# A macaron of attention and mixture-of-experts layers: the first grouped FFN in parts of 12, 12 and 8 token tiles, moments of the second attention between its slot tiles, and the expert search's counts in BF16

## The chip, the core and the metric

The kernel runs on one core of a Trainium2 chip. The metric is the device time of one execution in microseconds (us); the median of several executions is compared. PE is the matrix engine, PEld its weight load, DVE the vector engine, ACT the scalar engine, POOL the general engine that here mostly issues indirect DMAs, SP the engine that issues the other DMAs. All data are FP32 unless said otherwise.

## What is computed

4096 tokens (8 sequences of 512) of 256 numbers pass through six residual layers, in this order:

```python
x = x + 0.5 * ffn0(layernorm(x))   # 8 experts choose 512 tokens each of every 2048
x = x + attn0(layernorm(x))        # rope, 16 heads of 16, causal
x = x + 0.5 * ffn0(layernorm(x))
x = x + 0.5 * ffn1(layernorm(x))   # each token chooses 4 of 16 experts, plus a shared FFN
x = x + attn1(layernorm(x))        # 16 heads of 64, with its own inner residual
x = x + 0.5 * ffn1(layernorm(x))
```

In `ffn0` each expert takes the tokens with its highest scores (`top_k` over the tokens, for each half of the batch), runs them through 256-1024-256 with a GELU and adds them back weighted. In `ffn1` each token takes 2 of 4 groups of experts and then the 4 best experts:

```python
scores = softmax(x @ gate_w.T)
group_scores = scores.reshape(T, 4, 4).max(-1)
_, gidx = top_k(group_scores, 2)            # the others are masked
_, indices = top_k(masked, 4)
a = silu(x @ w1[e]) * (x @ w3[e])           # 256 -> 128
y = sum over the 4 experts of c[t, e] * (a @ w2[e])
z = (silu(x @ ws1) * (x @ ws3)) @ ws2       # shared, 256 -> 256 -> 256
```

## The kernel before

The 4096 tokens are 32 token tiles of 128 rows. The residual `x` stays in SBUF for the whole kernel. Six stages follow one another: `ffn0` until 583 us, `attn0` until 1285, `ffn0` again until 1838, `ffn1_before` until 2300, `attn1` until 3550, `ffn1_after` to the end. Within a stage the order of each engine's instructions is written out by hand (`manual_schedule`): instructions stand on each engine in the order of the Python calls, and the engines are strict queues. So what a change moves in the program moves on every engine that it touches.

**The search in `ffn0`.** The 512 best scores of each expert are found by a search for the threshold, two bits of the score a round (`search`, 8 and then 7 rounds). The scores lie as 128 rows of 256, 16 rows for each expert. In a round DVE compares all scores with two of three thresholds `thr` (L362, the results `junk` are thrown away, the counts go to `r`), ACT does the third by a sign; a matmul with the 0/1 matrix `same` sums the counts over the rows of an expert (`total`, L350, output `cnt`); DVE prepares `here` (L377) and `base` (L379), then turns the counts into a digit (`hit`, L384), the new thresholds (`thr`, L389) and the value found so far (`at`, L391). After the last round, ties are settled by two scans along the rows (`inc`, L421 and L428), and a matmul with `before` adds up the rows ahead of each row (`off`). `ffn0` normalizes its token tiles in groups of four (L254); some of these rows are POOL's.

**Layer norm.** `ln_moments` (L168, L169) takes mean and variance of one tile on DVE; `ln_finish` (L176 and on) turns the variances of several tiles into `rstd`, with a square root on ACT in the middle. The rows are then normalized one tile at a time.

**The grouped FFN** (`Grouped`, used as #1 before and #2 after the second attention). Tokens are sent to slots in HBM that are sorted by expert, 144 tiles of 128 slots. The tokens are handled in parts; #1 has four of 8 token tiles, #2 has three of 12, 8 and 12.

- `prepare(h)` works on part h: moments, finish, rows (`rows`, L1406, output `wide`), then for each group of four tiles the transposes (`tp`, L1687), the logits, and the way back to rows (L1708, L1713).
- `route(h)` takes the scores, the groups, the four experts and each row's slot, in one chain of DVE operations over all tiles of the part, with a few small matmuls (L1480, L1488, L1568) and ACT operations (L1444 the exponential) between.
- `send` (L1416) then issues four indirect DMAs for each token tile from POOL, one for each chosen expert; each moves 128 rows (128 KB) to their slots. A send waits until the send before the previous one has landed, so two are under way.
- `shared(g)` is the shared FFN of a group of four tiles (L1763, L1774, L1785), its last operation adds to `x` (L1791). `Pump` holds its units and issues them one by one.
- `tile_steps` gives `step(i)`: one slot tile moves on through a pipeline of turn (`tpx`, L1831; `xT`, L1833), hide (`hs`, L1849; `sgs`, L1855; `as`, L1857), back (L1861) and give (`yps`, L1869; `ys`, L1877 on ACT or L1879 on DVE), and the result is stored to `ys_d`. `load` brings four slot tiles (`xs`) from HBM. A slot tile belongs to a part once no later part can put rows into it; `closed[h]` slot tiles are closed after part h, and a load of such tiles waits for all sends of parts up to h. The rest wait for the last part. `ready[h]` is the number of slot tiles after which all results of part h are stored.
- `collect` gives a list of steps; each one gathers the four results of a token tile (`yg`, L1600, indirect DMA on POOL, four under way) and adds, two tiles behind, what was gathered (L1619 on DVE).

In `ffn1_before` (#1) the parts 0 and 1 are prepared, routed and sent ahead of the slot tiles, with the shared groups 0 to 3 in between; then the closed slot tiles of parts 0 to 1, and then 2, run with the routing and sending of parts 2 and 3 and the shared groups 4 to 7 beside them. From the slot tile `ready[0] + 6` on, one element of `collect` goes with each slot tile, until the first two parts are added. What is left goes into `attn1`. The weights of `attn1` (four loads of 1 MB) are issued in the same loop, one every eighth slot tile.

`attn1` begins with `ln_range` over its first 12 token tiles, that is their moments and the finish, then rows (`xn`, L1072) and transposes (`tpn`, L1084).

In `ffn1_after` (#2) the last part is prepared and routed first, since the earlier parts were sent during `attn1`; the slot tiles follow, with gathers alternately one and two at a tile; at the end the shared groups that are left run with the rest of the gathers and the output's DMAs.

Of the kernel before, what the change touches and what calls it, by code (L numbers as in the profile page):

```python
# [61 lines left out]
class Kernel:  # L62
    def __init__(self, ctx, tc, w):
# [44 lines left out]
        self.same = const.tile([P, P], F32, name="same")  # L108
# [10 lines left out]
        self.before = const.tile([P, P], F32, name="before")  # L119
# [89 lines left out]
    def ffn0(self, n, beside, known=0):  # L209


        with ExitStack() as ctx:
            E = mybir.EngineType
            with self.tc.manual_schedule(engines={E.PE, E.DVE, E.Activation, E.Pool}):
                self._ffn0(ctx, n, beside, known)

    def _ffn0(self, ctx, n, beside, known):
# [30 lines left out]
        def rows(g):  # L248
            xn = xns[g] = work.tile([P, QT, D], F32, name="xn", bufs=3)
            for i in range(QT):  # L250
                t = g * QT + i

                engine = nc.gpsimd if i == 3 or i == 1 and not known else nc.vector
                engine.tensor_scalar(  # L254
                    xn[:, i, :], self.x[:, t, :], mv[:, t, 0:1], rstd[:, t : t + 1], ALU.subtract, ALU.mult
                )
# [95 lines left out]
        def search(vals, rounds, between):  # L352
# [3 lines left out]
            at = None  # L356
            for b in range(rounds - 1, -1, -1):
                v = work.tile([P, D], F32, name="v", bufs=4)
                nc.scalar.mul(v, vals, 0.25 ** (b + 1))
                r = work.tile([P, 3], F32, name="r", bufs=2)  # L360
# [4 lines left out]
                nc.scalar.activation(signs, v, AF.Sign, bias=thr[:, 2:3], accum_out=r[:, 2:3])  # L365
                cnt = psum.tile([P, 3], F32, name="cnt", tag="psI", bufs=1)
# [20 lines left out]
                if b > 0:  # L387
                    thr = work.tile([P, 3], F32, name="thr", bufs=2)
                    nc.vector.scalar_tensor_tensor(thr, self.signs, digit[:, 0:1], base, ALU.mult, ALU.add)  # L389
                at = work.tile([P, 1], F32, name="at", bufs=4)  # L390
                nc.vector.tensor_scalar(  # L391
                    at, here, digit[:, 0:1], 0.0 if b > 0 else 0.5, ALU.add, ALU.add
                )
            return at
# [15 lines left out]
        sums = pool.tile([P, 2], F32, name="sums")  # L410
# [15 lines left out]
        nc.vector.tensor_tensor(gt, gt, eq, ALU.add)  # L426
# [3 lines left out]
        total(off, self.before, inc[:, D - 1 : D])  # L430
# [190 lines left out]
    def _attn0(self, ctx, weights):  # L621
# [353 lines left out]
        with tc.manual_schedule(engines={E.PE, E.DVE, E.Activation}):  # L975
# [22 lines left out]
            for g in range(G):  # L998
# [12 lines left out]
                if half == 1 and b > 0 and g % 6 < QT:  # L1011

                    self.ln_moments(pool, self.stats, (b - 1) * QT + g % 6, 1)
# [9 lines left out]
                finish(1)  # L1023
                do(mid)
# [25 lines left out]
    def _attn1(self, ctx, weights, beside, after):  # L1050
# [9 lines left out]
        stats = self.ln_tiles(pool)  # L1060
# [194 lines left out]

        E = mybir.EngineType
        with tc.manual_schedule(engines={E.PE, E.DVE, E.Activation, E.Pool}):
            self.ln_range(pool, stats, 0, 3 * QT)
# [92 lines left out]
class Grouped:  # L1351
# [58 lines left out]
    def send(self, h, t, row, behind=None):  # L1410
# [4 lines left out]
        for r in range(TOPK):  # L1415
# [5 lines left out]
            before = self.sent[-2:-1]  # L1421
            for other in before:
                tc.add_manual_dep(inst, other.name, SYNC, reason="two transfers at a time")
# [214 lines left out]


# [75 lines left out]
    def prepare(self, h):  # L1715
# [3 lines left out]
        for t in range(a, b, 2):  # L1719
            k.ln_moments(self.rpool, self.stats, t, 2)  # L1720
            yield
        k.ln_finish(self.rpool, self.stats, a, b - a)
        yield
        for t in range(a, b, 2):
            for i in range(t, t + 2):
                self.rows(k.nc.vector, self.xn[:, i, :], i)
            yield
# [12 lines left out]
    def send_next(self):  # L1740

        if self.waiting:
            h, t = self.waiting.pop(0)
            self.send(h, t, self.xn[:, self.base[h] + t, :], self.latest)
# [185 lines left out]
def ffn1_before(k, f):  # L1930
# [4 lines left out]
    with ExitStack() as ctx, k.tc.manual_schedule(engines={E.PE, E.DVE, E.Activation, E.Pool, E.SP}):  # L1935
# [6 lines left out]
        groups = [f.shared(g) for g in range(TT // QT)]  # L1942
        load, step, total = f.tile_steps()
        at = 0

# [3 lines left out]
        for h in range(2):  # L1949

            pair = groups[2 * h : 2 * h + 2]
            pump.feed(pair[0][0] + pair[1][0] + pair[0][1] + pair[1][1])
            routing, preparing, more = f.route(h), f.prepare(h + 1), True
            while more:
# [6 lines left out]
                more = f.send_next() or more  # L1961
        pump.flush()
        load(0)
        for h in (2, 3):
            one, two = groups[2 * h], groups[2 * h + 1]
            pump.feed(one[0] + two[0] + one[1] + two[1])
            routing, preparing, more = f.route(h), f.prepare(3) if h == 2 else iter(()), True
            while at < f.closed[h - 1] or more:
                if at < f.closed[h - 1]:
                    step(at)  # L1970
                    at += 1
                if at % 4 == 0 or at == f.closed[h - 1]:
                    pump.run(1)
                more = advance(routing, 2)
                more = advance(preparing, 1) or more
                pump.flush()
                more = f.send_next() or more
        while pump.units or pump.pending:
            pump.run(1)
        while at < f.closed[3]:  # L1980
            step(at)
            at += 1

        coming = f.collect()
        begin, weights = f.ready[0] + 6, None
        for i in range(at, total):
            step(i)
            if i >= begin and i % 8 == 0 and (weights is None or len(weights) < 4):
                weights = k.attn1_weights(weights)

            if i >= begin and len(coming) > (TT + 2 - f.base[2]) * TOPK:
                coming.pop(0)()
# [59 lines left out]
def ffn1_after(k, f, out):  # L2052
# [4 lines left out]
    with ExitStack() as ctx, k.tc.manual_schedule(engines={E.PE, E.DVE, E.Activation, E.Pool, E.SP}):  # L2057
# [7 lines left out]
        part = f.prepare(last)  # L2065
# [12 lines left out]

        def begin():

            t = (TT + 2) - -(-len(coming) // TOPK)
            return f.ready[sum(t >= b for b in f.base[1:-1])] + 6
# [23 lines left out]
        for i in range(total):  # L2106
# [10 lines left out]
            for _ in range(1 + i % 2):  # L2117
                if i >= begin():
                    coming.pop(0)()
        while pump.units or pump.pending:  # L2120
            pump.run(1)

            for _ in range(min((3, 3, 1, 1, 1, 1)[at % 6], len(coming))):
# [6 lines left out]
def tile_kernel(tc, w, out):  # L2130
    with ExitStack() as ctx:
# [11 lines left out]
        one = Grouped(k, 0, (8, 8, 8, 8))  # L2143
# [77 lines left out]
```

## Time and profile before

| | us |
|---|---|
| median of 3 runs | 3938.08 |
| the runs | 3942.79, 3936.67, 3938.08 |
| the profiled execution | 3943.58 |
| its span | 3941.9 |

The mean granted clock of PE in the profiled execution is 0.946 of full speed. By stage (busy us of the window):

| window, us | stage | length | PE | DVE | POOL |
|---|---|---|---|---|---|
| 58 to 113 | the search of the first `ffn0` | 55 | 15.73 | 40.88 | 8.56 |
| 113 to 583 | its experts | 470 | 461.00 | 82.60 | 164.84 |
| 583 to 1285 | `attn0` | 702 | 645.51 | 435.08 | 226.59 |
| 1285 to 1838 | second `ffn0` | 553 | 499.87 | 138.20 | 176.78 |
| 2300 to 3550 | `attn1` | 1250 | 1216.49 | 933.54 | 217.96 |
| 3550 to 3942 | `ffn1_after` | 392 | 353.67 | 190.68 | 181.07 |

In a line of a timeline the columns are: start, length, engine, line of the kernel, operation, output and inputs with shapes; in brackets, how long the engine had been idle and what released it. In a line of waits: engine and what it was about to do, what it waited for, then total us, number of times and the longest.

### The profile page before, as it was taken

The page shows a single profiled execution, that of the slowest core. Times are in us where ns is not written, and L with a number is a line of the kernel's source. Part 1 is how long each engine was busy: PE and PEld are TensorE (multiplying, and loading weights), DVE is VectorE, ACT ScalarE, POOL GpSimd, SP SyncE. Part 2 cuts the span into 40 slices and gives each one's busy share as a digit, 9 for nine tenths or more (in the row PEclk, how much of TensorE's full clock was granted, in tenths as well). Part 3 has the DMA queues.
Part 4 walks back from the last instruction along what each step waited for, and adds up shares of the span by engine and source line. Part 5 has one row for each costly group of instructions (what it writes and reads, how often), then busy time and mean ns, then how long its engine had stood idle before and what let it go on. Part 6 is the DMA issues. An engine that isn't in the chain of part 4 may idle for free.

```text
span 3941.9 us, 51214 instructions
## 1 busy us (share of the span) xinstructions
PE 3602.2 (91%) x17094; PEld 2121.6 (54%) x17094; DVE 2106.0 (53%) x5673; ACT 1492.4 (38%) x3437; POOL 1191.9 (30%) x1090
## 2 busy tenths in 40 slices
PE   4999988999998599998797989999999999998998
PEld 2666653444444266665366844554545545556775
DVE  6222116666665522212752668787687678764355
ACT  3222222444443322222243435454444444444442
POOL 2433423334230234331543512210100016302356
PEclk7999997999997699999798999999999999999999
DMA  6333326600110323324234811000000001115565
GB/s 202 68 77 67 75 55 222 204 25 14 26 26 23 105 65 75 80 53 130 90 117 158 279 52 31 27 18 1 1 1 1 1 11 57 41 33 168 165 212 159
DMA packets 262993, 316.62 MB, mean 80 GB/s; under 512 B 31696, under 2 KB 232784, under 8 KB 262480
## 3 DMA queue, kind: packets, MB, share of 16 engines
q1 hardware_dynamic: 213584, 212.12, 16.9%
q0 software_dynamic: 49152, 101.24, 10.6%
q8 instruction: 142, 2.33, 0.3%
q14 instruction: 115, 0.94, 0.1%
HBM read 157.81 MB, written 147.06 MB: 77 GB/s over the span
## 4 chain that ended last, share of the span: by engine, by line
PE 64%; issue 12%; DVE 11%; POOL 5%; ACT 4%; DMA 4%; POOLq 0%; SPq 0%; DVEq 0%; ACTq 0%
PE op L541 6%; PE hp L528 6%; PE zp L1189 5%; PE hs L1849 5%; PE sp L1141 5%; PE pq L1116 4%; PE tp L1175 4%; PE pv L1096 3%; PE yp L1208 3%; PE yps L1869 3%; PE hp L1763 3%; PE st L884 2%; POOL acc_d L548 2%; PE pp L736 2%; PE sp L843 2%
## 5 line engine op out<-in xcount | busy, mean ns | idle before, releaser
L1153 ACT ACTIVATE ex<-sp,nmax 128x512 f32<-128x512 f32 x512 | 344.8, 685 | 461.9 <-DVE nmax L1146 461.8
L541 PE MATMUL op<-w,hid 128*128 128x256 f32 x2048 | 456.2, 381 | 0.0
L528 PE MATMUL hp<-exT,w 128*128 128x512 f32 x1024 | 448.7, 597 | 0.0
L541 PEld LDWEIGHTS op<-w,hid 128*128 128x128 f32 x2048 | 385.9, 190 | 56.1 <-issue 7.6
L1600 POOL DMA_INDIRECT yg<-ys_d,slot x256 | 266.3, 1040 | 443.3 <-DVE x L1619 185.3
L548 POOL DMA_INDIRECT acc_d<-ob,idx x128 | 207.0, 1617 | 570.5 <-ACT ob L547 570.5
L546 DVE TENSOR_TENSOR ob<-op,b 128x256 f32<-128x256 f32 x128 | 54.3, 425 | 542.8 <-PE op L541 465.7
L1175 PEld LDWEIGHTS tp<-ident,ex 128*128 128x128 f32 x2048 | 227.3, 141 | 185.3 <-issue 104.1
L1849 PE MATMUL hs<-w_sb,xT 128*128 (+1 forms) x1152 | 306.3, 390 | 15.6 <-DVE as L1857 9.2
L528 PEld LDWEIGHTS hp<-exT,w 128*128 128x128 f32 x1024 | 193.9, 192 | 231.6 <-issue 229.7
L1146 DVE TENSOR_REDUCE nmax<-sp 128x2 f32<-128x1024 f32 x256 | 300.5, 1215 | 14.7 <-PE sp L1141 14.7
L532 ACT ACTIVATE hid<-hp,b 128x512 f32<-128x512 f32 x256 | 175.9, 687 | 322.7 <-PE hp L528 322.7
L1416 POOL DMA_INDIRECT slots_d<-wide,slot x176 | 174.5, 991 | 395.4 <-DVE lane L1555 217.3
L851 DVE CUSTOM_DVE_ANT_0 junk<-sp,mask 128x256 f32<-128x256 f32 (+3 forms) x512 | 249.2, 487 | 82.5 <-PE sp L843 59.8
L1175 PE MATMUL tp<-ident,ex 128*128 128x128 f32 x2048 | 279.7, 279 | 13.4 <-DVE eT L206 12.4
L1141 PE MATMUL sp<-qk,qk 64*128 64x512 f32 x1024 | 256.0, 618 | 2.2 <-ACT ex L1153 2.2
L1116 PE MATMUL pq<-xnT,wide 128*128 128x512 f32 x512 | 244.8, 603 | 8.1 <-ACT qk L1122 8.1
L1163 DVE TENSOR_SCALAR ex<-ex,rec 128x512 f32<-128x512 f32 x512 | 245.2, 521 | 8.9
L1189 PE MATMUL zp<-eT,v 128*64 128x512 f32 x1024 | 234.6, 599 | 0.0
L899 ACT ACTIVATE ex<-st 128x768 f32<-128x768 f32 (+1 forms) x192 | 168.5, 882 | 168.8 <-DVE st L897 166.1
L1849 PEld LDWEIGHTS hs<-w_sb,xT 128*128 128x128 f32 x1152 | 200.8, 194 | 38.1 <-ACT xT L1833 10.0
L547 ACT ACTIVATE ob<-ob,gate 128x256 f32<-128x256 f32 x128 | 65.0, 508 | 412.0 <-DVE ob L546 412.0
(344 smaller groups left out, 5735.4 us busy)
## 6 DMA issues: line engine op xcount, KB each, us to landing
xs<-slots_d SPq DMA_DIRECT2D x70, 512.0 KB, 5.5
ys_d<-ys SPq DMA_DIRECT2D x70, 512.0 KB, 3.3
w<-in_W SPq DMA_DIRECT2D x32, 1024.0 KB, 6.1
slots_d<-mask SPq DMA_DIRECT2D x8, 2304.0 KB, 13.1
ys_d<-mask SPq DMA_DIRECT2D x8, 2304.0 KB, 16.0
w_sb<-in_w SPq DMA_DIRECT2D x24, 512.0 KB, 6.5
xn_d<-xn SPq DMA_DIRECT2D x16, 512.0 KB, 3.3
acc_d<-x SPq DMA_DIRECT2D x8, 1024.0 KB, 5.5
```

What stands on the lines that cost most here:

```text
L528: nc.tensor.matmul(hp, lhsT=w1[:, c, f * P : f * P + P], rhs=exT[e][:, c, h * CH : h * CH + CH], start=(c == 0), stop=(c == DC - 1),)
L541: nc.tensor.matmul(op, lhsT=hid[h][:, f, i * P : i * P + P], rhs=w2[:, f, :], start=(f == 0), stop=(f == FC - 1),)
L548: inst = nc.gpsimd.indirect_dma_start(out=acc_d[:, :], out_offset=bass.IndirectOffsetOnAxis(ap=idx[:, e, st : st + 1], axis=0), in_=ob, in ...
L851: nc.vector.tensor_tensor_reduce(out=junk[:, :wd], in0=sps[h // 2][:, h % 2, at : at + wd], in1=mask[:, S - wd :], scale=1.0, scalar=NEG, ...
L1116: nc.tensor.matmul(pp, lhsT=(wq, wk)[a][:, k, c * P : c * P + P], rhs=seq[b]["xnT"][:, k, :], start=(k == 0), stop=(k == DC - 1),)
L1141: nc.tensor.matmul(sp[:, j, :], lhsT=q[r, qt * P : qt * P + P], rhs=k[r, :], start=True, stop=True)
L1146: nc.vector.tensor_reduce(m, sp, AX.X, ALU.max, negate=True)
L1153: nc.scalar.activation(ch["ex", 2 * half + i][:, j, :], sps[i][:, j, :], AF.Exp, bias=nmax[i][:, j : j + 1], accum_out=sums[i][:, j : j + 1],)
L1175: nc.tensor.transpose(tp[:, k, :], ch["ex", qt][:, j, k * P : k * P + P], self.ident)
L1189: nc.tensor.matmul(zp[DK1 * j : DK1 * j + DK1, :], lhsT=seq[b]["v", h][:, k, at : at + DK1], rhs=ch["eT"][:, j, k, :], start=(k == 0), sto ...
L1600: inst = nc.gpsimd.indirect_dma_start(out=self.y[t, r], out_offset=None, in_=self.k.ys_d[:, :], in_offset=bass.IndirectOffsetOnAxis(ap=sel ...
L1849: nc.tensor.matmul(hp.rearrange("p a i -> p (a i)"), lhsT=st[j]["xT"][:, c, :], rhs=self.w13[:, st[j]["e"], c, :].rearrange("p e i -> p (e ...
```

## The change

- In `ffn0` the counts `r`, the sums and the matrices `same` and `before` become BF16 (whole numbers up to 256). `at` is computed by a function `late` that is called after the next round's two compares rather than before them. The sum of each row for `off` comes from the operation that adds `eq` to `gt` rather than from the scan behind it. In the first `ffn0` the second row tile of groups 5 and on is DVE's rather than POOL's.
- In `attn0` the moments for the second `ffn0` stand later in a step.
- The first `Grouped` has parts of 12, 12 and 8 tiles. Closed slot tiles become 33 and 65 (before 17, 33 and 49), `ready` becomes 81, 128 and 144 (before 65, 96, 144 and 144). Parts 0 and 1 with shared groups 0 to 5 stand ahead of the slot tiles, and their sends are `alone`: the first send of a token tile waits for all four of the tile before, the other three wait for none.
- Gathers in `ffn1_before` go when `asked` allows it, one at a slot tile and two at each fourth. The moments of `attn1`'s first 12 tiles are taken as soon as a pair of tiles has all its results; `attn1` only finishes them.
- The moments of tiles 20 to 27 for the last stage are placed in `attn1`, and `prepare(last)` is told so (`known`). The last stage's gathers go one at a slot tile, and at the end two, two, one, one, one, one.

```diff
-        self.same = const.tile([P, P], F32, name="same")
+        self.same = const.tile([P, P], BF16, name="same")
-        self.before = const.tile([P, P], F32, name="before")
+        self.before = const.tile([P, P], BF16, name="before")
...
-                engine = nc.gpsimd if i == 3 or i == 1 and not known else nc.vector
+                engine = nc.gpsimd if i == 3 or i == 1 and not known and g < 5 else nc.vector
...
-                r = work.tile([P, 3], F32, name="r", bufs=2)
+                r = work.tile([P, 3], BF16, name="r", bufs=2)
...
+                if late is not None:
+                    at = late()
                 cnt = psum.tile([P, 3], F32, name="cnt", tag="psI", bufs=1)
                 total(cnt, self.same, r)
...
-                at = work.tile([P, 1], F32, name="at", bufs=4)
-                nc.vector.tensor_scalar(
-                    at, here, digit[:, 0:1], 0.0 if b > 0 else 0.5, ALU.add, ALU.add
-                )
-            return at
+                def late(here=here, digit=digit, half=0.0 if b > 0 else 0.5):
+                    at = work.tile([P, 1], F32, name="at", bufs=4)
+                    nc.vector.tensor_scalar(at, here, digit[:, 0:1], half, ALU.add, ALU.add)
+                    return at
+            return late()
...
-        sums = pool.tile([P, 2], F32, name="sums")
+        sums = pool.tile([P, 3], BF16, name="sums")
...
-        nc.vector.tensor_tensor(gt, gt, eq, ALU.add)
+        nc.vector.scalar_tensor_tensor(gt, gt, 0.0, eq, ALU.add, ALU.add, accum_out=sums[:, 2:3])
...
-        total(off, self.before, inc[:, D - 1 : D])
+        total(off, self.before, sums[:, 2:3])
```

```diff
@@ attn0
-                if half == 1 and b > 0 and g % 6 < QT:
-                    self.ln_moments(pool, self.stats, (b - 1) * QT + g % 6, 1)
                 one, mid, two = units[g % 6]
...
                 finish(1)
+                if half == 1 and b > 0 and g % 6 < QT:
+                    self.ln_moments(pool, self.stats, (b - 1) * QT + g % 6, 1)
@@ attn1
+        for t in range(after.base[-2], TT - QT, 2):
+            own.setdefault(NC * (t // QT + 1) + 3 + t % QT, []).append(moments(front.pool, after.stats, t))
...
-            self.ln_range(pool, stats, 0, 3 * QT)
+            self.ln_finish(pool, stats, 0, self.BEGIN)
@@ Grouped
-            before = self.sent[-2:-1]
+            before = self.sent[-2:-1] if not alone else self.sent[-TOPK:] if r == 0 else []
...
+    def asked(self, coming):
+        t = (TT + 2) - -(-len(coming) // TOPK)
+        return self.ready[sum(t >= b for b in self.base[1:-1])] + 6
...
-    def prepare(self, h):
+    def prepare(self, h, known=0):
...
+        c = max(a, known)
+        pieces = [(a, c), (c, b)] if a < c else [(c, b)]
+        for first, end in pieces:
+            if first == c:
+                for t in range(first, end, 2):
+                    k.ln_moments(self.rpool, self.stats, t, 2)
+                    yield
+            k.ln_finish(self.rpool, self.stats, first, end - first)
             yield
+            for t in range(first, end, 2):
+                for i in range(t, t + 2):
+                    self.rows(k.nc.vector, self.xn[:, i, :], i)
+                yield
```

```diff
@@ ffn1_before
+        def feed(h):
+            groups = [f.shared(g) for g in range(f.base[h] // QT, f.base[h + 1] // QT)]
+            pump.feed(groups[0][0])
+            for one, two in zip(groups, groups[1:]):
+                pump.feed(two[0] + one[1])
+            pump.feed(groups[-1][1])
...
-        for h in range(2):
-            pair = groups[2 * h : 2 * h + 2]
-            pump.feed(pair[0][0] + pair[1][0] + pair[0][1] + pair[1][1])
+        for h in range(last):
+            feed(h)
             routing, preparing, more = f.route(h), f.prepare(h + 1), True
...
-                more = f.send_next() or more
+                more = f.send_next(True) or more
         pump.flush()
         load(0)
-        for h in (2, 3):
...
-                more = advance(routing, 2)
-                more = advance(preparing, 1) or more
+        feed(last)
+        routing, more = f.route(last), True
+        while at < f.closed[1] or more:
...
+            more = advance(routing, 4)
...
-        coming = f.collect()
-        begin, weights = f.ready[0] + 6, None
+        def moments(t):
+            if t < k.BEGIN and t % 2:
+                k.ln_moments(f.rpool, k.stats, t - 1, 2)
+
+        coming, weights = f.collect(moments), None
         for i in range(at, total):
             step(i)
-            if i >= begin and i % 8 == 0 and (weights is None or len(weights) < 4):
+            if i >= f.asked(coming) and i % 8 == 0 and (weights is None or len(weights) < 4):
                 weights = k.attn1_weights(weights)
-            if i >= begin and len(coming) > (TT + 2 - f.base[2]) * TOPK:
-                coming.pop(0)()
+            for _ in range(1 + (i % 4 == 0)):
+                if i >= f.asked(coming):
+                    coming.pop(0)()
+        while len(coming) > (TT - k.BEGIN) * TOPK:
+            coming.pop(0)()
@@ ffn1_after
-        part = f.prepare(last)
+        part = f.prepare(last, TT - QT)
...
-            for _ in range(1 + i % 2):
-                if i >= begin():
-                    coming.pop(0)()
+            if i >= f.asked(coming):
+                coming.pop(0)()
...
-            for _ in range(min((3, 3, 1, 1, 1, 1)[at % 6], len(coming))):
+            for _ in range(min((2, 2, 1, 1, 1, 1)[at % 6], len(coming))):
@@ tile_kernel
-        one = Grouped(k, 0, (8, 8, 8, 8))
+        one = Grouped(k, 0, (12, 12, 8))
```

## The prediction

> **What bounds the kernel now.** I read the busy table first, then the slices, then the chain of waits.
>
> ```profile
> PE 3602.2 (91%) x17094; PEld 2121.6 (54%) x17094; DVE 2106.0 (53%) x5673; ACT 1492.4 (38%) x3437; POOL 1191.9 (30%) x1090
> ...
> PE   4999988999998599998797989999999999998998
> ...
> PE 64%; issue 12%; DVE 11%; POOL 5%; ACT 4%; DMA 4%; POOLq 0%; SPq 0%; DVEq 0%; ACTq 0%
> ```
>
> TensorE is the bound nearly everywhere, so a change can only win in the slices that are not 9: the start, slice 13 (the second expert choice), slices 19 to 22 (the first grouped FFN) and the end. The diff edits just these places. The grouped FFN, in windows of 62 and three times 100 us (columns: window, length, busy time of PE, PEld, DVE, ACT, POOL with counts, granted clock, DMA share, GB/s):
>
> ```profile
> 1838.00:1900.00 62.00, 36.87 (x112) 20.00 (x113) 41.42 (x159) 12.42 (x19) 8.09 (x8) 0.75 0.61 197
> 1900.00:2000.00 100.00, 80.54 (x276) 45.13 (x274) 62.82 (x245) 34.84 (x76) 55.23 (x56) 0.85 0.31 108
> 2000.00:2100.00 100.00, 94.97 (x443) 69.31 (x442) 49.65 (x191) 45.26 (x151) 48.11 (x49) 1.00 0.44 149
> 2100.00:2200.00 100.00, 72.92 (x391) 60.44 (x390) 30.67 (x93) 36.46 (x135) 34.45 (x35) 0.86 0.57 187
> ```
>
> With the row from 2200 on, PE is busy 376 of 462 us. What ended its idle time from 1838 to 2310 (total us, times, longest):
>
> ```profile
> PE tpx L1831 <- DMA xs<-slots_d: 26.5, 2, 26.3
> PE tp L1687 <- issue: 17.4, 1, 17.4
> PE tp L1687 <- DVE wide L1406: 9.9, 4, 4.9
> PE tpn L1084 <- DVE xn L1072: 8.9, 1, 8.9
> ```
>
> The first row is one hole: PE has run its 49 closed slot tiles by 2101.7 and can't start the 50th until 2128.0, because the load behind it waits for every send of the last part. Those sends go until then (columns: start, length, engine, line, ...; idle before and its releaser):
>
> ```profile
> 2119.74 0.98 POOL L1416 DMA_INDIRECT slots_d<-wide,slot  x1 [0.41 <-DMA slots_d<-wide,slot]
> 2121.04 0.98 POOL L1416 DMA_INDIRECT slots_d<-wide,slot  x1 [0.32 <-DMA slots_d<-wide,slot]
> ```
>
> So the last send, 2122, and the 99 slot tiles left behind it set the end of the stage: (2290.6 − 2128.0)/99 = 1.64 us each. That is the number on which the change turns.
>
> **Part 1: parts of 12, 12 and 8.** Slot tiles and sends stay 148 and 128; the tiles that may run ahead of the last part become 65 instead of 49. Three clocks have to be followed.
> First send: before, 1888.7. Preparing four more tiles costs DVE 4 × (0.53 moments + 0.45 rows) = 4 and PE's turns and logits about 3; the routing's operations on 192 elements take 0.35 where those on 128 took 0.29, some 4 us over the chain. First send at about 1900.
> Sends, by POOL: before, two are under way at a time, and a tile of four took (1934 − 1888.7)/8 = 5.7 us in the first part and (2069.7 − 2008.9)/8 = 7.6 beside slot tiles. After, the first two parts send four and then wait for all four: three steps of 1.29, then issue to landing. Quiet, one such wait was 2.74, so 6.6 us a tile; beside slot tiles a third send waited until its pair had landed 3.7 us after issue (typical; 4.8 for 2008.87 to 2013.65), so 3 × 1.29 + 3.7 = 7.6. Part 0: 12 × 6.6 = 79, done at 1979. Part 1: 12 × 7.6 = 91, done at 2071. Part 2, in pairs with its routing long done (it starts at about 1984 at twice the pace; before it took 1958 to 2009): 32 sends at the last part's 50 us, 2123, usable at 2128.
> This is where a rule is weighed. The Trainium skill, DMA: Bandwidth & Descriptors, section Anatomy of one DMA (SWDGE path), prices such a transfer at 2.0 us plus bytes over 436 GB/s: 128 KB give 2.3, a tile 6.2 and both parts 149 us instead of 170, the last send 21 us earlier. The row with traffic says 3.7; I take the row, since slot tiles run beside part 1, and keep the rule for the good end.
> PE: shared groups 0 to 5 (before 0 to 3) stand ahead of the first slot tile and keep PE until about 1979, the first load lands at 1984. 33 tiles × 1.63 = 54, the shared work fed in between 23, routing waits 3: 2063. Then it waits for part 1's sends plus 5 for landing and load, 2076: a new hole of 13. 32 tiles: 2128. There the last part is ready too, and 83 tiles × 1.65 follow: 2265 to 2267. Against 2290.6 that is −24: the last send lands when it did, with 16 fewer tiles (16 × 1.64 = 26) behind it, and the hole of 26.3 has been spent on earlier holes.
> Sixteen ys copies move from DVE to ACT, at 45% in that window: nothing. One table load set fewer: within the routing's waits.
> Gathers and adds now go at 1.25 a tile, 65 in all (64 before). A gather takes POOL 1.31 with its gap; 1.25 × 1.31 = 1.64 against a step of 1.65: full but carried. If adds wait for rows, as in the stage at the end, they hold DVE in front of the gate product `as`; by that stage's rate (9.2 us of PE waits over some 60 tiles) up to +9. I take +0, keeping +9 for the range.
>
> **Part 2: moments for attention 1.** The hole of 8.9 (2290.6 to 2299.4) holds twelve moments, 12 × 0.53 = 6.4, and the finish, 2.5. The moments go between slot tiles, where DVE is 63% busy (62.95 of 100 from 2200): −6.4. Without that cover they would come back whole. The weights of attention 1 (4 loads of 1 MB on SP) start at tile 88 rather than 72, still some 70 us ahead of their use: 0.
> Stage and start together: −30, bounds −45 and −10.
>
> **Part 3: the search for the threshold in the expert choice.** One round (period 58.70 to 61.00, DVE alone):
>
> ```profile
> 58.49 0.21 DVE L391 TENSOR_SCALAR at<-here,digit 128x1 f32<-128x1 f32 x1
> ...
> 59.62 0.15 DVE L377 TENSOR_SCALAR here<-at 128x1 f32<-128x1 f32 x1
> 59.81 0.22 DVE L379 SCALAR_TENSOR_TENSOR base<-signs,here,steps 128x3 f32<-128x3 f32 x1
> 60.45 0.16 DVE L384 SCALAR_TENSOR_TENSOR hit<-cnt,reach 128x3 f32<-128x3 f32 x1 [0.42 <-PE cnt L350]
> ```
>
> `at` leaves the path between `thr` and the compares (−0.09 to −0.13) for the 0.42 in which DVE waits for the count. The count (0.56 for two f32 passes, weights 0.50 ahead) gets one BF16 pass, near 0.3 by half the row: −0.28. Then DVE's own at, here, base end it. I take −0.31 a round, bounds −0.10 (no gain from the type) and −0.40; 15 rounds: −4.6. The matmul `off` (0.58, and 0.68 of DVE waiting) goes beside the scan: −0.55. TensorE, VectorE and the sums stay as they are elsewhere. −5.2 for each of two stages, and −1 for three rows off POOL (1.25 there, 0.45 on DVE) at the end of the first: −11, bounds −14 and −4.
>
> **Part 4: attention 0.** 28 moments move from ahead of a step's reductions to behind its softmax. PE waited 14.7 us for DVE at `st` in this stage, a few of them beside a moment: −2, bounds −6 and +1.
>
> **Part 5: the last stage.** Attention 1 has PE 97% busy and takes the moments of tiles 20 to 27 for nothing. Preparing: rows 20 to 27 start at once, the moments of 28 to 31 stand behind them, about 0. The gathers slow from 1.5 to 1 a tile. What that pace cost (PE, then DVE, waits from 3550 on):
>
> ```profile
> PE hs L1849 <- DVE as L1857: 9.2, 6, 2.6
> ```
> ```profile
> DVE x L1619 <- DMA yg<-ys_d,slot: 37.2, 36, 3.4
> ```
>
> At one a tile POOL needs 1.31 of 1.65, so the 9.2 go. But three gathers more are left for the end, which POOL sets (gathers 1.325 apart until 3936, landing, add and store until 3941.9), and the drain is slower (8 in 6 units instead of 10): +3. Sum −6, bounds −10 and +6.
>
> **Sum:** −30 − 11 − 2 − 6 = −49. Against the profiled execution, 3943.6: 3894.6. It lies 5.5 above the median of the runs shown, 3938.1; the forecast is 3889.
>
> **Rivals.** About 8 us (0.2%) is what this measurement can tell from no change.
> *The sends become the bound (slower).* Place: the wait for all four sends at each tile's first. Price: 24 tiles, so 24 us for each us of P, the time of a tile of four; my mean P is 7.1. The whole gain is gone from P = 7.1 + 49/24 = 9.1, a landing of 5.3. For: 4.8 was seen, four sends contend where two did. Against: quiet landing is 2.7, and DMA is 31 to 44% busy there. At P = 9.6: +60 on the forecast, 3949. Chance 0.15.
> *Half is given back.* P = 7.7 (+14) and adds that wait at 1.25 a tile (+9) or a drain that costs: 3889 + 26 = 3915. For: POOL is full there. Against: at one a tile no add waited before. Chance 0.23.
> *No new hole.* By the rule's 2.3 the sends end 21 us earlier, PE never waits for part 1, and the stage ends up to 14 sooner: 3875. For: in the first part the row agrees with the rule. Chance 0.14.
> *My sum*, 3889, own range 3880 to 3900: 0.48.
>
> **Numbers.** Faster takes my sum, no new hole and most of the half: 0.48 + 0.14 + 0.16 = 0.78; same 0.07; slower 0.15. The range, 3862 to 3936, leaves out the sends' rival and little below.
>
> **What would show it.** First send near 1900; last near 2123 while 83 tiles follow; one PE wait for `xs` of some 13 at 2063 rather than 26 near the end; the wait at `tpn` 2.5; rounds of 2.0; `hs` waiting for `as` under 2 in the last stage. Sends 9 us a tile, or `x` waiting for `yg` in the first grouped FFN, would make me wrong.

## The result and the profile after

The changed kernel takes 3916.5 us (median of 6), the kernel before, run beside it, 3941.7. The ratio is 0.9933, 95% interval 0.9915 to 0.9952. That is 25 us by the medians, where 49 were forecast. The profiled execution of the changed kernel took 3919.9 us. Its page (busy time of each engine; the span in 40 slices, in tenths; the chain that ended last):

```profile
PE 3580.3 (91%) x17052; PEld 2104.1 (54%) x17052; DVE 2088.3 (53%) x5564; ACT 1493.7 (38%) x3450; POOL 1188.6 (30%) x1087
...
PE   3999988999999499997788999999999999998997
...
PE 64%; issue 13%; DVE 10%; POOL 5%; DMA 4%; ACT 4%; SPq 0%; POOLq 0%; DVEq 0%; ACTq 0%
```

The weak slices are still there, 14 and 19 to 22. Where the time went is read from marks that both traces have. The last two columns are the same two kernels on another chip (runs c_before and c_after below).

| from, to (us between the marks) | before | changed | before, other chip | changed, other chip |
|---|---|---|---|---|
| first count of the first search to `off` | 38.8 | 33.5 | 38.8 | 33.5 |
| first `st` of attention 0 to the second search | 657.4 | 648.1 | 659.0 | 648.6 |
| second search to `off` | 38.4 | 33.5 | 38.5 | 33.5 |
| last `op` of the second `ffn0` to first `tpn` (first grouped FFN) | 466.4 | 462.2 | 474.5 | 475.8 |
| of it: first send to last send | 232.4 | 245.0 | 231.1 | 245.3 |
| of it: PE's restart behind the last send to the last `yps` | 162.6 | 140.9 | 171.5 | 153.4 |
| of it: last `yps` to first `tpn` | 8.9 | 2.9 | 8.9 | 3.9 |
| last product of attention 1 to the end | 388.5 | 387.8 | 420.4 | 392.3 |
| of it: slot tiles, first `tpx` to last `yps` | 298.2 | 288.5 | 321.2 | 292.5 |
| of it: from there to the last gather | 70.5 | 78.6 | 79.0 | 79.0 |

So the two searches gave 10, attention 0 gave 9, the first grouped FFN 4 instead of 30, the last stage 1. Of the 4 us, 6.0 come from the moments of attention 1 (the row that ends at `tpn`); the parts of 12, 12 and 8 for themselves cost 1.8. On the other chip the last stage gave 28 and the first grouped FFN cost 1.

The first grouped FFN by its phases: ahead of part 0's sends, part 0's sends, part 1's, the last part's, the rest (columns as in the windows before; granted clock, DMA share and GB/s at the end):

```profile
1826.00:1880.00 54.00, 40.83 (x116) 20.28 (x116) 34.24 (x114) 13.83 (x21) 1.17 (x2) 0.80 0.60 167
1880.00:1968.00 88.00, 65.06 (x217) 34.71 (x216) 61.36 (x211) 17.06 (x28) 48.97 (x50) 0.88 0.22 78
1968.00:2061.00 93.00, 78.63 (x352) 58.59 (x352) 37.19 (x136) 40.21 (x131) 45.58 (x46) 0.92 0.46 148
2061.00:2131.00 70.00, 54.59 (x290) 45.35 (x291) 9.23 (x32) 34.78 (x128) 31.45 (x32) 0.89 0.60 190
2131.00:2272.00 141.00, 136.56 (x726) 112.21 (x724) 78.82 (x239) 67.15 (x246) 63.12 (x61) 0.99 0.72 230
```

What ended PE's idle time in that stage, and at the start of attention 1:

```profile
PE tpx L1852 <- DMA xs<-slots_d: 23.5, 4, 12.2
PE tp L1702 <- issue: 20.7, 1, 20.7
PE yp L1806 <- DVE x L1812: 18.3, 8, 6.7
...
PE tpn L1091 <- DVE xn L1079: 3.0, 1, 3.0
```

One hole of 26.3 has become two, 12.2 ahead of part 1's tiles and 10.2 ahead of the last part's. The hole at `tpn` went from 8.9 to 3.0 as forecast. The sends, quiet in part 0 and beside slot tiles in the last part (start, length, engine, line, ..., idle before and its releaser):

```profile
1882.49 0.98 POOL L1426 DMA_INDIRECT slots_d<-wide,slot  x1 [0.30 <-issue]
1885.68 0.98 POOL L1426 DMA_INDIRECT slots_d<-wide,slot  x1 [2.21 <-DVE hots L1598]
...
2063.95 0.98 POOL L1426 DMA_INDIRECT slots_d<-wide,slot  x1 [0.51 <-DMA slots_d<-wide,slot]
2069.64 0.98 POOL L1426 DMA_INDIRECT slots_d<-wide,slot  x1 [4.70 <-DMA slots_d<-wide,slot]
```

The first pair is the wait for all four: 3.2 us from one issue to the next, at nearly every tile of part 0 with the same 2.2 of idle (the releaser that is named had long been done; it is the DMAs). The second pair is a send of the last part, beside running slot tiles. It waits for the send before the previous one, issued at 2062.45, and so goes 7.2 us after that one. A round of the search, DVE alone:

```profile
57.63 0.48 DVE L365 TENSOR_SCALAR_CACHE_REDUCE junk<-v,thr 128x256 f32<-128x256 f32 x1
...
58.56 0.21 DVE L399 TENSOR_SCALAR at<-here,digit 128x1 f32<-128x1 f32 x1
58.80 0.15 DVE L382 TENSOR_SCALAR here<-at 128x1 f32<-128x1 f32 x1
58.99 0.22 DVE L384 SCALAR_TENSOR_TENSOR base<-signs,here,steps 128x3 f32<-128x3 f32 x1
59.13 0.15 DVE L389 SCALAR_TENSOR_TENSOR hit<-cnt,reach 128x3 f32<-128x3 f32 x1
```

`hit` no longer waits for the count; the round takes 2.04 us (57.63 to 59.67) instead of 2.30.

### The profile page after: what moved, and what is told of

Read it like the earlier page. It is cut to its first block, busy times and chain, and to the rows that moved or that the text cites. A ratio compares the mean times of both kernels' runs of the same rounds, so it can differ in the third digit from the quotient of the medians.

```text
span 3918.2 us, 51040 instructions
## 1 busy us (share of the span) xinstructions
PE 3580.3 (91%) x17052; PEld 2104.1 (54%) x17052; DVE 2088.3 (53%) x5564; ACT 1493.7 (38%) x3450; POOL 1188.6 (30%) x1087
## 3 DMA queue, kind: packets, MB, share of 16 engines
q8 instruction: 142, 2.33, 0.3%
## 4 chain that ended last, share of the span: by engine, by line
PE 64%; issue 13%; DVE 10%; POOL 5%; DMA 4%; ACT 4%; SPq 0%; POOLq 0%; DVEq 0%; ACTq 0%
PE op L548 6%; PE hp L535 6%; PE zp L1196 5%; PE hs L1870 5%; PE sp L1148 5%; PE pq L1123 4%; PE tp L1182 4%; PE pv L1103 3%; PE yp L1215 3%; PE hp L1784 3%; PE st L891 3%; PE yps L1890 2%; POOL acc_d L555 2%; PE pp L743 2%; PE sp L850 2%
## 5 line engine op out<-in xcount | busy, mean ns | idle before, releaser
L858 DVE CUSTOM_DVE_ANT_0 junk<-sp,mask 128x256 f32<-128x256 f32 (+3 forms) x512 | 249.5, 487 | 78.6 <-PE sp L850 55.7
L1878 DVE TENSOR_TENSOR as<-sgs,hs 128x128 f32<-128x128 f32 x288 | 82.6, 287 | 261.7 <-ACT sgs L1876 261.5
```

Of the source, the lines that this page charges most:

```text
L858: nc.vector.tensor_tensor_reduce(out=junk[:, :wd], in0=sps[h // 2][:, h % 2, at : at + wd], in1=mask[:, S - wd :], scale=1.0, scalar=NEG, ...
```

## The experiments

The question was why the first grouped FFN gave 4 us and not 30. Theory A: the sends are its bound, and the changed rule (four, then wait for all four) made them slower. Theory B: the holes only move, with PE's front work and traffic setting the pace. The runs went to three further chips: A (e1_pairs to e4_counts_f32), B (c_after, c_before, e5_tail, e6_pairs_tail; the other chip of the table) and C (e7_control to e10_old_moments). There the kernel before took 3999, 3985 and 4003 us instead of 3942, and the changed one, which ran on B and C, 3934 and 3939: it is 51 and 63 us faster there, and 25 on the first chip. So runs are compared with the changed kernel on the same chip, or by stages. None of the edits below ran on the first chip.

**Sends in pairs again** (all else as changed):

```diff
-                more = f.send_next(True) or more
+                more = f.send_next() or more
```

> The changed kernel, but the sends of the first two parts go two at a time as before (the alone rule undone). Theory A, the sends are the bound of the first grouped FFN: part 0 takes 12 x 5.7 = 68 instead of 12 x 7.07 = 85 us, part 1 some 12 x 7.6 = 91 instead of 96; the last send comes about 20 us earlier, at 2103 instead of 2123.5, the PE wait of 12 for part 1 is gone and that of 10 for the last part is under 3: 15 to 20 us faster than the changed kernel, near 3898. Theory B, the holes only move (front work of PE and traffic set the pace): the same within 4 us, 3912 to 3920.

Measured: 3918.6 us; from first to last send 231.0 us (245 with the rule); PE's two holes at `xs`, from turn to turn less a step, 4.6 and 9.5 us (15.8 and 10.4 in the changed kernel's trace). The changed kernel was not on that chip, so it was repeated with a control:

> The changed kernel, unaltered, as the control of this comparison: 3916 to 3934 by the chip. From the end of the second expert choice to the first turn of attention 1: 462 (first chip) to 476 us.

> The changed kernel with its sends in pairs in all parts, now beside the changed kernel on one chip. Theory A: 15 us faster than the control (last send 14 us earlier after the first, the first PE wait for xs 5 instead of 16); the stage takes 461 to 464 us. Theory B, the gain of the first comparison belonged to the chip: within 4 us of the control.

Measured: control 3939.5 (3931 to 3941), pairs 3922.2 (3920 to 3927): 17 us faster. The stage took 461.9 us against the control's 484.7 (475.8 in the other trace of the changed kernel). PE's waits in the stage, first the control, then pairs:

```profile
PE tpx L1852 <- DMA xs<-slots_d: 24.0, 2, 12.1
```
```profile
PE tpx L1852 <- DMA xs<-slots_d: 6.8, 2, 5.9
```

The wait for slots falls by 17.2, as does the time. Theory A holds: the sends are the bound, and on these chips the rule "four, then wait" costs some 17 us. Most of it is lost in the quiet part: part 0's sends take 86.5 us with the rule and 72.8 in pairs, part 1's 96.8 and 91.0, the last part's, in pairs in both, 64.8 and 66.0. A hole of 5.9 ahead of the last part's tiles stays.

**The whole first grouped FFN undone**: that of before with its parts of 8, 8, 8, 8, sends in pairs and one gather a tile, and the moments at the start of attention 1, in an otherwise changed kernel (its loops are those of before; two of the lines):

```diff
-        one = Grouped(k, 0, (12, 12, 8))
+        one = Grouped(k, 0, (8, 8, 8, 8))
...
-            self.ln_finish(pool, stats, 0, self.BEGIN)
+            self.ln_range(pool, stats, 0, self.BEGIN)
```

> The changed kernel with the whole first grouped FFN of before (parts 8, 8, 8, 8, sends in pairs, one gather a tile) and the moments of attention 1 at its start again; the search, attention 0 and the last stage stay changed. From the two traces the stage and its start give 4 us (the first turn of attention 1 is 24.9 earlier, the end of the second expert choice already 20.6): 2 to 8 us slower than the changed kernel, near 3921. Rival, the parts give what was forecast (30): 3945.

Measured: 3933.5 us, beside pairs' 3918.6 on the same chip; the stage took 479.1 us. With the changed parts and the changed rule for the sends it took 480.9 on that chip (in the kernel with FP32 counts below, which is the same there), with pairs 464.4. So with the changed rule the whole new stage, its moments included, is worth nothing there (one trace each); with pairs it is worth 15.

**Four sends always under way**:

```diff
-            before = self.sent[-2:-1] if not alone else self.sent[-TOPK:] if r == 0 else []
+            before = (self.sent[-4:-3] if self.n == 0 else self.sent[-2:-1]) if not alone else self.sent[-TOPK:] if r == 0 else []
...
-                more = f.send_next(True) or more
+                more = f.send_next() or more
```

> The changed kernel, but every send of the first grouped FFN waits only for the one four before it, so four are always under way. Theory A: a tile of four takes 4 x 1.29 = 5.2 us of issue, in all parts; the last send is 40 us or more earlier, or as early as the routing of the last part allows (its slots stood at 1999); no PE wait for xs over 2 us; 20 to 25 us faster than the changed kernel, near 3893. Theory B, four at once beside slot tiles contend and land later: issue stalls of 3 to 5 us stay, last send within 8 us of 2123, no faster than the changed kernel.

Measured: 4005.5 us. Neither theory had this. The stage took 546 us, 65 more than with the changed rule on that chip and 82 more than with pairs. The sends went 1.29 us apart as hoped while they ran, but the other engines stopped, and then POOL had to wait for them: from first to last send it was 237.5 us, only 8 to 10 less than with the changed rule. The timeline around 1915 (weight loads left out of what is shown):

```profile
1898.63 0.66 PE L1702 MATMUL tp<-ident,wide 128*128 128x128 f32 x4 [1.58 <-issue]
...
1915.12 0.98 POOL L1426 DMA_INDIRECT slots_d<-wide,slot  x1 [0.30 <-issue]
1915.63 0.42 DVE L1812 SCALAR_TENSOR_TENSOR x<-yp,x 128x256 f32<-128x256 f32 x1 [19.70 <-remote]
...
1926.13 0.58 ACT L1705 COPY xnT<-tp 128x512 f32<-128x512 f32 x1 [20.44 <-remote]
1926.77 1.12 PE L1702 MATMUL tp<-ident,wide 128*128 128x128 f32 x4 [19.91 <-ACT xnT L1705]
```

POOL issued on to 1922.85 without a wait, and DVE and ACT stood for 20 us each, PE behind ACT. The profile calls their releaser "remote", which means that it found no instruction that ended close enough before. The packed trace tells more: each of these waits of over 1 us, in this run and in all others, is for the semaphore that only PE's matmuls raise, and it rises late. The copy at 1926.13 is let go by a rise at 1926.11; the turns that it waits for, in the order of the rises, are those of 1898.63, recorded as done at 1899.29. The four rises from 1905.08 to 1928.23 come 9 to 27 us behind their matmuls' recorded ends. What ended ACT's and DVE's waits between 1830 and 2125:

```profile
ACT xnT L1705 <- remote: 46.3, 4, 20.4
```
```profile
DVE x L1812 <- remote: 29.1, 2, 19.7
```

With pairs no such wait is in that stretch; there POOL pauses for about 0.4 us or more at every second send.

**Counts in FP32**, with the late `at` and the new `off` kept:

```diff
-        self.same = const.tile([P, P], BF16, name="same")
+        self.same = const.tile([P, P], F32, name="same")
...
-                r = work.tile([P, 3], BF16, name="r", bufs=2)
+                r = work.tile([P, 3], F32, name="r", bufs=2)
```

(`before` and `sums` likewise.)

> The changed kernel with counts, sums and their matrices in FP32 again, at still late and off still beside the scan. If the type gives most of the gain of a round, rounds go back from 2.0 to about 2.2 us: +0.2 x 15 x 2 = +6 us. If the late at gives most: +1 or less.

Measured: 3946.7 us, and by the marks, first count to `off`, 37.7 and 37.8 us, against 33.5 in BF16 and 38.8 and 38.4 before. The type gives 4.3 of a search's gain, the rest 1. The round is at 2.30 again, DVE waiting 0.17 for the count where it waited 0.42: `at` fills the wait, but saves nothing ahead of the compares, since from `thr` to the next compare it is 0.35 us with `at` between them (58.35 to 58.70) and without (57.28 to 57.63).

**The changed kernel and the kernel before, unaltered, on one other chip**:

> The changed kernel itself, unaltered, beside the others on one chip, so that they can be compared with it. Theory A (sends bound): the last send some 245 us after the first, PE waits of about 12 and 10 for xs. If the 83 tiles behind the last send take 157 us here, as in the kernel with FP32 counts, and not 141 as in its first profile, the difference belongs to the chip and not to an edit.

> The kernel before, profiled on this chip. In the last comparison its time was 3999 where it had been 3938 elsewhere. If engines stand still while POOL sends without a pause (as they did for 20 us with four sends under way), the stage of the first grouped FFN is longer by most of the difference and its waits name no engine; if the chip is slower throughout, every stage is longer by 1 to 2%.

Measured: 3934.0 and 3983.6 us. The 83 tiles behind the last send took 153.4 us here: that is the chip's, not an edit's. The kernel before is not slower throughout: its search, attention 0 and experts agree with the first chip within 2 us a mark. It loses 9 in the tiles with gathers of the first grouped FFN and 32 in the last stage, 23 of these in the slot tiles, where it gathers at 1.5 a tile. So neither reading of the expectation holds.

**Gathers of the last stage at 1.25 a tile**:

```diff
-            if i >= f.asked(coming):
-                coming.pop(0)()
+            for _ in range(1 + (i % 4 == 0)):
+                if i >= f.asked(coming):
+                    coming.pop(0)()
```

> The changed kernel, but the gathers of the last stage go at 1.25 a slot tile instead of 1. Theory A, the end is POOL's: in the trace of the changed kernel POOL waited 53 us for x in that stage at one gather in 1.64 us, while 1.31 suffice; 19 steps more are done beside the slot tiles, 40 instead of 59 are left, and the end is then PE's: last gather before PE's last product, 10 to 15 us faster, near 3904. Theory B, the adds wait for rows and hold DVE ahead of the gate product: PE waits for as come back with 5 to 9 us and the gain is under 5.

Measured: 3947.8 us, 14 slower than the changed kernel. The slot tiles took 307.3 instead of 292.5 us, the end 74.5 instead of 79.0. In the tiles with gathers, from 3640 on, PE's waits name no row that is late: none over 3.2 us in all, and `as` for 0.2. Neither theory forecast a loss, and theory B's wait for `as` is not there: tiles with two or more gathers in a row took up to 5.0 us instead of 1.63. What held them is in the last section.

> Both: sends in pairs in all parts and the gathers of the last stage at 1.25. If the two gains are real and separate: 14 from the sends and 10 to 15 from the end, 24 to 29 us faster than the changed kernel on this chip. If pairs only move the hole: no more than the tail alone.

Measured: 3925.0 us, 22.7 faster than the run before it, 9 faster than the changed kernel. The stage of the first grouped FFN took 460.8 (476.7 without pairs), the last 402.1 as in the run before it. By the stages the effects are separate; the forecast failed by the sign of the second.

**Three edits together**: pairs, gathers in the first grouped FFN at one a tile, and the quicker end.

```diff
-            for _ in range(min((2, 2, 1, 1, 1, 1)[at % 6], len(coming))):
+            for _ in range(min((3, 3, 1, 1, 1, 1)[at % 6], len(coming))):
```

> Sends in pairs, gathers in the first grouped FFN at one a slot tile instead of 1.25, and three, three, one, one, one, one at the end instead of two, two, one, one, one, one. Pairs give 15, the slower gathers 4 to 8 (the 83 tiles behind the last send then take 145 us or less where the control takes 153), the quicker end 5 to 8 (51 gathers at 1.33 to 1.4 instead of 1.54): 24 to 30 us faster than the control. If POOL's unbroken gathers hold back the shared FFN's instructions at the end, PE's end moves out and that part gives nothing: 19 to 23.

Measured: 3923.0 us (3913 to 3933), 16 faster than the control and no faster than pairs alone. By stages: the tiles behind the last send took 145.8 (control 159.2, pairs 155.8), so the slower gathers give 10 beside pairs, and the stage is down to 453.1. The end gives it back: from the last slot tile PE needs 90.2 us instead of 63.1, and the last gather comes after 93.9 instead of 79.5. There, for ACT and then PE:

```profile
ACT xnT L1705 <- remote: 32.0, 3, 15.2
```
```profile
PE hp L1784 <- ACT xnT L1705: 21.6, 4, 10.3
```

Asked to go faster, POOL issues up to 20 gathers at most 1.6 us apart. ACT's copies of the shared FFN's transposes wait 15 us for PE's semaphore, whose rises come up to 11.8 us late; and in the end the gathers, which need adds to free their buffers, come later too.

**Moments of attention 0 back in place, and gathers in the first grouped FFN at one a tile**:

```diff
@@ attn0
+                if half == 1 and b > 0 and g % 6 < QT:
+                    self.ln_moments(pool, self.stats, (b - 1) * QT + g % 6, 1)
                 one, mid, two = units[g % 6]
...
                 finish(1)
-                if half == 1 and b > 0 and g % 6 < QT:
-                    self.ln_moments(pool, self.stats, (b - 1) * QT + g % 6, 1)
```

> Two edits in stages apart, read from the trace: the moments in attention 0 ahead of the reductions again, and gathers at one a tile in the first grouped FFN (sends stay four at a time). If the place of the moments is what shortened attention 0 by 9 to 10 us (first product to the second search, 648 before 657 to 659), it goes back to 657; if it was the granted clock, it stays at 648 or 640. If 1.25 gathers a tile cost what I suspect, the 83 tiles behind the last send take 4 to 8 us less than in the control; if not, the same within 2.

Measured in one execution: attention 0 took 658.0 us, with 648.6 in the changed kernel; it is the moments. PE waited here as before the change, and then, in the changed kernel:

```profile
PE st L891 <- DVE top L858: 14.7, 21, 3.2
```
```profile
PE st L891 <- DVE top L858: 9.3, 10, 3.2
```

In three traces with the changed place (640.3 in the control) attention 0 ran 8 us shorter still, at a granted clock of 0.93; that is not the edit. At about the same clock, 0.90 to 0.91, the three traces with the old place have 657 to 659 and the eight others with the new one 648 to 649. The tiles behind the last send took 146.0 us, 7 to 13 less than the controls.

## Why the prediction was right in its sign and half right in its size

- **First grouped FFN and its start: −30 forecast, −4.2 measured.** Counted from the end of the second `ffn0`, 25.8 us are missing, all of them in the parts: they were to give 24 and cost 1.8. The first send is right (10.4 later against 11.3 forecast). The step that failed is "Sends, by POOL". Part 0: "Quiet, one such wait was 2.74, so 6.6 us a tile"; measured 3.2 a wait and 7.2 a tile on average. Part 1: 7.6 forecast, 8.0 measured. Last part: "32 sends at the last part's 50 us"; measured 62. Together it is 245 us from first to last send against 223 (the forecast's own terms add up to 220): 22 us. Part of the third term was misread: the last part's sends took 53.6 us in the kernel before, not 50. The rest is an error of kind. In the kernel before the last part sent half of its rows while PE stood in the hole: its first 16 sends took 32 us beside slot tiles (2067.5 to 2099.5), its other 16, with PE standing from 2101.7 on, 21.6 to the last issue. The hole is now filled with slot tiles, and 62 fits the pace beside them, twice 32; that alone was not tested. The other 4 us are the 83 tiles: 1.70 each against 1.65.
- The signs to watch were in part met by luck. The hole ahead of part 1's tiles has its forecast size (12.2 against 13), but the sends' end and PE's arrival both come some 11 us late there. The second hole, 10.2 ahead of the last part's tiles, was not forecast. `x` did wait for `yg` in this stage, 11.7 us of DVE in nine waits, which was named as a sign of being wrong; PE lost 2.6 to it at `as`.
- The rule of the Trainium skill weighed there (DMA: Bandwidth & Descriptors, Anatomy of one DMA), 2.0 us plus bytes over 436 GB/s, gives 2.3 for a transfer; the quiet wait for four is 3.2 from issue to next issue, and beside slot tiles 7.2 was seen. The row was right to be preferred, and not taken far enough: a wait of 7.4 stood in the trace before as well (2068.76 to 2076.18), where 4.8 was named as seen.
- The rival "half is given back" has the measured number, 3915 against 3916.5, and its P of 7.7 (7.6 measured). Its terms make some 20 of its 26 us: 12 by P, 2.6 at `as`, 5 at the drain. That the whole agrees to 1.5 us is luck: the 12 us more of the last part's sends are in no rival, and the 7 us more that attention 0 gave hide a good part of them. The rival "the sends become the bound" is right in kind, but its deciding point (P = 9.1) was not reached. That the faster send rule would be the old one was not among the cases.
- **Moments ahead of attention 1** (in the −30): −6.4 forecast, −6.0 measured, the mechanism as described.
- **The search**: −5.2 each forecast, −5.3 and −4.9 measured. Its split was wrong: `at` gives nothing, the type 4.3. Three rows off POOL: −1 forecast, nothing seen within the marks' 2 us.
- **Attention 0**: −2 forecast, −9.3 measured. "A few of them beside a moment" was the mis-sized term: 11 of the 21 waits at `st`, 5.4 us of idle time, went with the moments; 3.8 us of the rest is in PE's busy time, and why is open.
- **The last stage**: −6 forecast, −0.7 measured. The tiles gave 9.7 (9.2 forecast); the end cost 8.1 (3 forecast): 54 gathers start behind the last `yps` where it was 48, and they go 1.48 us apart on average instead of 1.38. On chip B the stage gives 28: there 1.5 gathers a tile cost 23 us of slot tiles, which no row of the first trace could show.

A version that beats both kernels is the changed one with sends in pairs: 3922.2 against 3939.5 and 4002.7 on one chip. By the stages, one gather a tile in the first grouped FFN with the changed end would give 10 more; that kernel was not run.

## What to carry to other kernels

When a transfer holds the compute engine up, ask how fast the transfers will go once the hole is filled: their speed in the hole is not the speed that they will have. Outside the first chip, the best pace of POOL's indirect DMAs here was not the one at which POOL is always busy. The price of such a pace differed by tens of microseconds from chip to chip, so a pace should be chosen on more than one.

## What had not been expected of the hardware

When POOL issues indirect DMAs with hardly a pause, PE's semaphore rises late, and ACT, DVE and then PE itself wait. A rise is called late here when it comes over 0.3 us after the last recorded end of a matmul that raises it. In the last stage's slot tiles, from 70 us after the first turn on, the packed traces show:

| run | chip | gathers a tile | late rises | their sum, us | all slot tiles, us |
|---|---|---|---|---|---|
| before | first | 1.5 | 0 | 0 | 298.2 |
| changed | first | 1 | 0 | 0 | 288.5 |
| c_before, the kernel before | B | 1.5 | 68 | 53 | 321.2 |
| e5_tail, gathers at 1.25 | B | 1.25 | 44 | 45 | 307.3 |
| e6_pairs_tail, and sends in pairs | B | 1.25 | 71 | 53 | 306.8 |
| c_after, the changed kernel | B | 1 | 9 | 15 | 292.5 |
| e7_control, the changed kernel | C | 1 | 10 | 5 | 292.2 |

The 83 tiles of the first grouped FFN show the same: at 1.25 gathers a tile 29 and 31 late rises on chip C (e7_control, e8_pairs_again), at one a tile 25 and 15 (e9_combined, e10_old_moments), and none on the first chip. In attention 1, where POOL is busy for some 220 of 1250 us, there is at most one in any trace. ACT's semaphore has no late rise in any of these stretches. (In each trace of the other chips some 200 of 4000 rises are not recorded, some of them in attention 1, where this makes none late.) So the slower tiles go with late rises, and both with POOL's pace; that the late rises are the cause is read from the waits of the long stalls, and no run changed them alone.

The long stalls are the extreme. In the run with four sends under way the late rises end at 1926.11 and 1928.23, after POOL's last send of the row at 1922.85; in the run with three edits, at 3865.45 and 3867.60 after POOL's last gather at 3865.28, and at 3901.48 after 3901.15. The data engines are not full in such a stall. The same 34 us in the run with four under way and with pairs (columns as in the windows before):

```profile
1893.00:1927.00 34.00, 6.06 (x27) 4.24 (x27) 3.36 (x11) 1.75 (x3) 23.63 (x24) 0.60 0.27 97
```
```profile
1893.00:1927.00 34.00, 31.06 (x104) 16.02 (x104) 19.88 (x63) 10.36 (x16) 21.97 (x22) 0.94 0.24 86
```

One candidate is the supply of instructions. The Trainium skill, Runtime: NRT & Kernel Launch, section Instruction fetch mechanics, says that instructions stream in in blocks of 16 KiB over a DMA queue and that this is mostly hidden. The page of the changed kernel fits the size, 142 packets and 2.33 MB in the first of two instruction queues, 16.4 KB each:

```profile
q8 instruction: 142, 2.33, 0.3%
q14 instruction: 114, 0.93, 0.1%
```

The traces speak against it. In the run with four under way no packet of either queue starts between 1911 and 1971, while the waits end at 1915.61 and 1926.11; in the run with three edits none starts between 3845 and 3880, while the wait ends at 3865.45. The ends of matmuls are modelled in the profile, so whether the matmuls themselves end late or only their signal comes late is not told. What POOL's indirect DMAs and PE share stays open, as does why the first chip shows none of it.
